# Edge attention on a graph: batches of seven chunks, three buffers of gathered rows, four chunks in one stationary operand

## The chip, the cores and the metric

The kernel runs on one core of a Trainium2 chip. The metric is the device time in microseconds (us), the median of several runs. The engines are named as in the profile: PE is TensorE (PEld its weight loads), DVE is VectorE, ACT is ScalarE, POOL is GpSimd, SP is SyncE. L509 is line 509 of the kernel before.

## What is computed

One attention layer over a graph of 12,500 nodes and 412,500 edges, with 4 heads of 32 columns. The edges come sorted by target node.

```python
h = jnp.maximum(_layernorm(x, axis=-1), 0.0)
h = (h @ W_node.T).reshape(num_nodes, H, HD)             # 12500 x 4 x 32
e = (edge_features @ W_edge.T).reshape(num_edges, H, HD)
h_src = h[src]
h_tgt = h[tgt]
att = jnp.sum(jnp.concatenate([h_src, h_tgt, e], axis=-1) * a, axis=-1)
att = jnp.where(att > 0, att, 0.2 * att)
m = jnp.maximum(segment_max(att, tgt), 0.0)
ex = jnp.exp(att - m[tgt])
denom = segment_sum(ex, tgt) + (num_edges - deg)[:, None] * jnp.exp(-m)
w = ex / denom[tgt]
h_prime = segment_sum(w[:, :, None] * h_src, tgt)
return x + h_prime.reshape(num_nodes, H * HD)
```

The costly part is `h_src`: for each of the 412,500 edges a row of the node table is fetched, weighted by the edge's attention and summed into its target's row.

## The kernel before

First the kernel builds a table in DRAM, one row of 144 f32 values (576 bytes) for each node: four heads of 35 columns (32 features, and columns for sums and maxima, the last of them the source's attention logit) and four logits that the target side uses. Then it goes over the edges.

An edge **chunk** is 896 edges (7 tiles of 128), 461 chunks in all, the last with 3 tiles. A **batch** is CB = 8 chunks (4 pairs), 58 batches in all. The batch loop stands at L775 to L808. In round b it issues, in this order:

- `index(b+2)`: the end points of the edges of a later batch, by a DMA on SP's queue.
- `load(b+1)` (L474 to L502): on SP's queue the edge features `eft` (1792 KB), the edges' targets `mem` (896 KB) and eight small loads `twb` of the target logits.
- `gather(b+1)` (L504 to L512): on POOL, first a copy of one column from `sums` to `gate` (L507), then 56 indirect DMAs (L509), each of which fetches 128 rows of the table into `hs`. There are two buffers of `hs`, for odd and even batches, so the rows of batch b+1 overwrite those of batch b-1. The copy is what makes POOL wait: `sums` is written when the last group of batch b-1 has come out of PE.
- `weigh(b)` (L564 to L592): waits for the rows of batch b. DVE takes the source logits out of `hs` by a transpose (L568), adds them to the logits `z` in PSUM (L576), takes the leaky maximum (ACT L577, DVE L578), runs two scans that find each segment's maximum (L580, L582), ACT takes the exponential (L586), and two transposes (L590, L591) put the weights into PSUM and the maxima back into `hs`.
- `load_pen(b+1)`: penalties that mark segment borders, for the scans.
- `scatter(b)` (L594 to L615): DVE multiplies the rows of each chunk by its weights (L605). Then the sums are matmuls (L613): the stationary operand is a 0/1 membership matrix `hot` of 32 target rows for each of up to G = 3 chunks (128 x 96), the moving one the weighted rows of these chunks (128 x 420), accumulated over 7 tiles into `pa`, of which PSUM holds two buffers. A batch is three groups of 3, 3 and 2 chunks. A group's products between different chunks are not used. In `collect` (L619 to L636) ACT copies the used 32 x 35 pieces out of `pa` (L636), and with the last group of a batch it writes `sums` (L623).
- `begin(b+1)` (L532 to L562): DVE compares the targets (L536), PE computes the logits `z` of the next batch from `eft` (L541, 8 matmuls) and from `mem` and `twb` (L545, 4 matmuls), DVE builds the next `hot` (L549 to L560).
- every two batches `merge` (L638 to L683): DVE joins the two batches' 16 partial results and adds them to `acc`. Some batches also finish a part of the output (L723 to L763). After batch 3 the kernel counts windows (`count_windows`) once.

In the last two batches each group holds one chunk (`step`). Each engine works through its instructions in the order in which they were issued, so POOL issues all gathers of a batch, then meets the next gate. An f32 matmul appears in the trace as two records of PE.

Of the kernel before, what the change touches and what calls it, by code (L numbers as in the profile page):

```python
# [22 lines left out]
K = 64  # L23
# [8 lines left out]
CB = 2 * SB  # L32
NBT = -(-NCH // CB)
NSC = NBT * SB
NC2 = NSC * 2
COLS = NSC * CT
# [4 lines left out]
G = 3  # L41
# [5 lines left out]
R = CB * H  # L47
# [4 lines left out]
ROW = EROW + H  # L52
BUF = max(CE, MC * 2 * AW, CB * H * AW)
# [8 lines left out]
def tiles_of(sc):  # L62

    return [T if c < NCH - 1 else LAST for c in (2 * sc, 2 * sc + 1) if c < NCH]
# [39 lines left out]
def kernel(  # L104
# [41 lines left out]
    nid = const.tile([P, NC2 // 4], F32, name="nid")  # L146
# [10 lines left out]
    left_row = const.tile([1, NSC], F32, name="left_row")  # L157
    down = const.tile([1, NSC], F32, name="down")
    nc.gpsimd.iota(down, pattern=[[-1, NSC]], base=NSC, channel_multiplier=0,
                   allow_small_or_imprecise_dtypes=True)  # L160
# [5 lines left out]
    sums = const.tile([W, 1], F32, name="sums")  # L166
# [12 lines left out]
    def index(b):  # L179
        t = indices.tile([P, SB, 2, CT], I32, name="ends")  # L180
        nc.sync.dma_start(t.rearrange("p j w t -> p (j w t)"), ends[:, b * SB * 2 * CT:(b + 1) * SB * 2 * CT])
        return t


    with (
# [216 lines left out]
        for s in range(2):  # L402
            for j in range(SB):
                at = (2 * j + s) * H
                nc.vector.tensor_copy(wa3[s * K:(s + 1) * K, j, at:at + H], pe[s * K:(s + 1) * K, :])
# [42 lines left out]
        for a in range(4):  # L448
            r = slice(a * W, (a + 1) * W)
            nc.vector.tensor_scalar(nid[r, :].rearrange("p (b k) -> p b k", k=2),  # L450
                                    top[r, :].rearrange("p (b a k) -> p b a k", a=4, k=2)[:, :, a, :], rcol[r, :],
                                    None, op0=OP.add)
# [4 lines left out]
    even = stack.enter_context(tc.tile_pool(name="even", bufs=1))  # L457
# [3 lines left out]
    bank = ps.tile([P, T * R + W + GB * 4 + NC2 // 4], F32, name="exr")  # L461
# [12 lines left out]
    def load(s):  # L474

        c0 = s.b * CB
        s.eft = work.tile([P, SB, CE], F32, name="eft")
        nc.sync.dma_start(s.eft, ef[s.b * SB:(s.b + 1) * SB, :, :].rearrange("j p e -> p j e"))
        s.mem = work.tile([P, 2, CE], F32, name="mem")
        rows = dstc[c0:c0 + CB, :].rearrange("(a k) e -> a (k e)", k=2)  # L480
# [12 lines left out]
        s.tiles = []  # L493
        for t in range(T):
            for sc in range(s.b * SB, (s.b + 1) * SB):
                held = tiles_of(sc) + [0, 0]
                for c in range(2):
                    i = (sc - s.b * SB) * CT + c * T + t
                    if t < held[c]:
                        s.tiles.append(i)  # L500
                    else:
                        nc.vector.memset(s.hs[:, i, :], 0.0)  # L502

    def gather(s, sums=None):  # L504

        if sums is not None:
            nc.gpsimd.tensor_copy(gate[:W, :], sums)  # L507
        for i in s.tiles:
            by_itself(nc.gpsimd.indirect_dma_start(  # L509
                out=s.hs[:, i, :], out_offset=None, in_=table[:, :],  # L510
                in_offset=bass.IndirectOffsetOnAxis(ap=s.ends[:, i // CT, 0, i % CT:i % CT + 1], axis=0)),
                f"rows{s.b}", row_sems, row_done, s.b % ROWSEMS)  # L512
# [14 lines left out]
    def load_pen(s):  # L527
        s.pen = work.tile([R, CE + 1], F32, name="pen")
        rows = pens[s.b * CB:(s.b + 1) * CB, :]
        nc.sync.dma_start(s.pen, rows[:, None, :].to_broadcast([CB, H, CE + 1]))  # L530

    def begin(s):  # L532
# [14 lines left out]
        dk = work.tile([P, SB * CT], I32, name="dk")  # L547
        dst = s.ends[:, :, 1, :]
        nc.vector.tensor_scalar(dk.rearrange("p (j t) -> p j t", t=CT), dst, W - 1, None, op0=OP.bitwise_and)  # L549

        key = work.tile([P, SB * CT], F32, name="key")
        nc.vector.tensor_tensor(
            key.rearrange("p (j c t) -> p j c t", c=2, t=T), dst.rearrange("p j (c t) -> p j c t", t=T),
            floor[:, s.b * CB:(s.b + 1) * CB].rearrange("p (j c) -> p j c", c=2)[:, :, :, None]
            .to_broadcast([P, SB, 2, T]), op=OP.subtract)
        nc.vector.tensor_scalar(key, key, float(W), float(W), op0=OP.is_ge, op1=OP.mult)
        nc.vector.tensor_tensor(key, key, dk, op=OP.add)
        for q0 in range(0, s.chunks, 2):
            k = key[:, q0 * T:q0 * T + CT].rearrange("p (q t) -> p q t", t=T)
            nc.vector.tensor_tensor(hot[:, :, q0:q0 + 2, :].rearrange("p t q r -> p q t r"),  # L560
                                    rows_ps[:, None, None, :].to_broadcast([P, 2, T, W]),
                                    k[:, :, :, None].to_broadcast([P, 2, T, W]), op=OP.is_equal)  # L562

    def weigh(s):  # L564
# [3 lines left out]
        nc.vector.transpose(zst.rearrange("p t i -> p (t i)"),  # L568
                            s.hs[:, :, :EROW].rearrange("p (q t) (h k) -> p t q h k", t=T, h=H)[:, :, :, :, AW - 1])
# [17 lines left out]
        for g in range(NQT):  # L587
# [3 lines left out]
        nc.vector.transpose(s.hs[:, :, :EROW].rearrange("p (q t) (h k) -> p t q h k", t=T, h=H)[:, :, :, :, AW - 1],  # L591
                            both[:, 1, :, :].rearrange("p t r -> p (t r)"))  # L592

    def scatter(s):  # L594


        by_chunk = s.hs[:, :, :EROW].rearrange("p (q t) k -> p q t k", t=T)
        held = [n for j in range(SB) for n in tiles_of(s.b * SB + j)]
        step = G if s.b + 2 < NBT else 1
        for q0 in range(0, s.chunks, step):  # L600
            w = min(step, s.chunks - q0)
            for q in range(q0, q0 + w):
                n = held[q]
                rows = by_chunk[:, q, :n, :].rearrange("p t (h k) -> p t h k", h=H)[:, :, :, :HB]
                nc.vector.tensor_tensor(  # L605
                    rows, rows, ex_ps[:, :n, q * H:(q + 1) * H, None].to_broadcast([P, n, H, HB]), op=OP.mult)
            pa = ps.tile([P, G * H * AW], F32, name="pa", bufs=2)

            n = held[q0 + w - 1]
            order = [0, *range(n, T if w > 1 else n), *range(1, n)]  # L610
            for i in order:
                v = w if i < n else w - 1
                nc.tensor.matmul(pa[:v * W, :v * H * AW], hot[:, i, q0:q0 + v, :].rearrange("p q r -> p (q r)"), by_chunk[:, q0:q0 + v, i, :],  # L613
                                 start=(i == order[0]), stop=(i == order[-1]))
            collect(s, q0, w, pa)  # L615
# [3 lines left out]
    def collect(s, q0, w, pa):  # L619

        first, last = merge_of(s.b)
        if s.b + 2 < NBT and q0 + w == s.chunks:
            nc.scalar.copy(sums, pa[:W, 0:1])  # L623
        if s.b == first and q0 == 0:
# [3 lines left out]
        for q in range(w):  # L628
            at = 1 + (s.b - first) * CB + q0 + q
            for h in range(H):  # L630
                to = merged["r"][h * W:(h + 1) * W, :, at]
                k = (q * H + h) * AW
                if s.b == NBT - 1 and q0 + w == s.chunks and h % 2:
                    nc.vector.tensor_copy(to, pa[q * W:(q + 1) * W, k:k + AW])
                else:
                    nc.scalar.copy(to, pa[q * W:(q + 1) * W, k:k + AW])  # L636
# [138 lines left out]
    with tc.manual_schedule():  # L775
        for b in range(-1, NBT):
# [37 lines left out]
    ps = stack.enter_context(tc.tile_pool(name="rest_ps", bufs=1, space=bass.MemoryType.PSUM))  # L814
    def window():
# [51 lines left out]
        nc.sync.dma_start(eft, ef[ds(sc, 1), :, :].rearrange("o p e -> p (o e)"))  # L867
        by_step = ends.rearrange("p (s w t) -> p s w t", w=2, t=CT)
        src_w = work.tile([P, CT], I32, name="src_w")
        nc.sync.dma_start(src_w, by_step[:, ds(sc, 1), 0, :])  # L870
        dw = work.tile([P, CT], I32, name="dst_w")
        nc.sync.dma_start(dw, by_step[:, ds(sc, 1), 1, :])
# [188 lines left out]
```

## Time and profile before

| what | value |
|---|---|
| runs: median (lowest to highest of 3) | 4826.44 us (4820.51 to 4826.88) |
| the profiled execution's own time | 4815.92 us |
| its span, first to last instruction | 4814.2 us |
| mean granted clock of TensorE | 0.643 |
| PE busy, records | 1946.2 us, 4305 |
| PE weight loads busy | 658.6 us |
| DVE busy | 1805.7 us |
| ACT busy | 719.1 us |
| POOL busy | 3073.5 us |
| matmuls of the sums (L613) | 2526 records, 967.1 us |
| matmuls of the logits (L541 and L545) | 928 and 464 records, 587.0 and 341.2 us |
| multiplying rows by weights (L605) | 461 of 1102 ns |
| gathers (L509) | 3223 of 948 ns |
| DMA traffic | 440.72 MB, mean 92 GB/s |

Lines of the profile are read so: a group's line gives engine, operation, the tiles written and read, the count, busy us and mean ns of one, and then the idle time of the engine just ahead of such instructions with what ended most of it. A timeline's line gives start and duration in us, engine, line, operation, shape and count, and in brackets the idle time before and what ended it.

### The profile page before, as it was taken

How to read it: one execution, taken by the hardware profiler on the slowest of the kernel's cores; microseconds unless marked ns; L12 is line 12 of the kernel's file. 1: busy time of each engine (PE TensorE's matmuls, PEld its weight loads, DVE VectorE, ACT ScalarE, POOL GpSimd, SP SyncE). 2: the span in 40 equal slices, each digit the busy share in tenths (PEclk: the TensorE clock that was granted, in tenths of full speed). 3: DMA queues.
4: the chain of work that ended last, by engine and by line, in shares of the span. 5: the costliest groups of instructions: out<-in, count | busy, mean ns of one | idle time of the engine just before them, and what ended most of it. 6: DMA issues, size and time to landing. Idle time of an engine off the chain costs nothing.

```text
span 4814.2 us, 21409 instructions
## 1 busy us (share of the span) xinstructions
PE 1946.2 (40%) x4305; PEld 658.6 (14%) x4305; DVE 1805.7 (38%) x3337; ACT 719.1 (15%) x2772; POOL 3073.5 (64%) x3333
## 2 busy tenths in 40 slices
PE   5334343433344335343434443434334433443353
PEld 3111111111011111110111111111111111110012
DVE  6242434242334332433343333424342434242425
ACT  5111111110111111111111111111111111110111
POOL 3666666666666666666666666666666666666662
PEclk8566666666666656665656665666566756666666
DMA  6332433333333333333333333333343333333431
GB/s 189 90 88 73 118 79 100 80 103 78 100 83 101 83 95 84 100 79 100 83 95 88 91 88 94 85 94 89 88 95 79 100 80 99 78 104 76 103 81 51
DMA packets 227639, 440.72 MB, mean 92 GB/s; under 512 B 85394, under 2 KB 135566, under 8 KB 227502
## 3 DMA queue, kind: packets, MB, share of 16 engines
q0 software_dynamic: 103136, 237.83, 21.8%
q1 hardware_dynamic: 111038, 194.10, 13.4%
q10 hardware_dynamic: 13328, 7.36, 0.5%
q14 instruction: 100, 0.82, 0.1%
q8 instruction: 37, 0.61, 0.1%
HBM read 423.75 MB, written 15.29 MB: 91 GB/s over the span
## 4 chain that ended last, share of the span: by engine, by line
issue 29%; another core or an unknown queue 27%; PE 22%; DVE 12%; ACT 8%; DMA 1%; DVEq 0%; SPq 0%; ACTq 0%; POOL 0%
PE pa L613 13%; PE z L541 6%; ACT r L636 4%; PE z L545 3%; DVE up L580 2%; DVE m L582 2%; ACT up L749 1%; DVE z L576 1%; ACT a L577 1%; ACT both L586 1%; DVE acc L683 1%; DVE a L583 1%; DVE up L664 1%; DVE hs L605 1%
## 5 line engine op out<-in xcount | busy, mean ns | idle before, releaser
L509 POOL DMA_INDIRECT hs<-table,ends x3223 | 3054.4, 948 | 1037.3 <-issue 1008.5
L613 PE MATMUL pa<-hs,hot 128*96 128x420 f32 (+2 forms) x2526 | 967.1, 549 | 1606.8 <-issue 1184.7
L560 DVE TENSOR_TENSOR hot<-exr,key 128x448 f32<-128x448 f32 x231 | 137.4, 621 | 2460.3 <-remote 2136.4
L541 PE MATMUL z<-eft,wa 128*32 128x384 f32 (+1 forms) x928 | 587.0, 695 | 913.6 <-issue 913.6
L636 ACT COPY r<-pa 32x35 f32<-32x35 f32 x1842 | 385.0, 209 | 2782.7 <-remote 1965.1
L613 PEld LDWEIGHTS pa<-hs,hot 128*96 128x96 f32 (+2 forms) x2526 | 445.1, 181 | 2152.8 <-issue 2044.2
L605 DVE TENSOR_TENSOR hs<-hs,exr 128x924 f32<-128x924 f32 x461 | 476.8, 1102 | 0.0
L545 PE MATMUL z<-mem,twb 128*32 128x512 f32 x464 | 341.2, 826 | 268.1 <-issue 268.1
L507 POOL COPY gate<-sums 32x1 f32<-32x1 f32 x56 | 9.9, 177 | 567.4 <-ACT sums L623 543.0
L541 PEld LDWEIGHTS z<-eft,wa 128*32 128x32 f32 x928 | 104.4, 117 | 1325.4 <-issue 1325.4
L576 DVE TENSOR_TENSOR z<-z,zst 32x224 f32<-32x224 f32 x232 | 89.8, 387 | 162.0 <-PE z L545 74.1
L586 ACT ACTIVATE both<-a 32x224 f32<-32x224 f32 x232 | 89.9, 388 | 370.7 <-DVE a L583 186.7
L536 DVE TENSOR_TENSOR mem<-mem,exr 128x896 f32<-128x896 int32 x116 | 120.4, 1077 | 65.5 <-issue 48.1
L577 ACT ACTIVATE a<-z 32x224 f32<-32x224 f32 x232 | 80.3, 346 | 418.0 <-issue 274.1
L545 PEld LDWEIGHTS z<-mem,twb 128*32 128x32 f32 x464 | 61.2, 134 | 585.3 <-issue 563.3
L683 DVE TENSOR_TENSOR acc<-acc,a 128x70 f32 x461 | 108.5, 235 | 33.8 <-issue 14.5
L580 DVE TENSOR_TENSOR_SCAN up<-pen,z 32x896 f32<-32x896 f32 x58 | 117.0, 2017 | 2.0
L582 DVE TENSOR_TENSOR_SCAN m<-pen,up 32x896 f32<-32x896 f32 x58 | 116.4, 2007 | 2.0
L588 DVE SCALAR_TENSOR_TENSOR both<-pen,m 32x224 f32<-32x224 f32 x232 | 88.7, 382 | 7.1 <-issue 4.8
L749 ACT COPY up<-a 32x224 f32<-32x224 f32 x208 | 70.7, 340 | 33.6 <-issue 23.3
L578 DVE TENSOR_TENSOR z<-z,a 32x896 f32<-32x896 f32 x58 | 63.0, 1087 | 24.5 <-issue 12.6
L583 DVE TENSOR_TENSOR a<-z,m 32x896 f32<-32x896 f32 x58 | 62.5, 1078 | 2.0
(142 smaller groups left out, 726.0 us busy)
## 6 DMA issues: line engine op xcount, KB each, us to landing
eft<-in_ef SPq DMA_DIRECT2D x58, 1792.0 KB
mem<-in_dstc SPq DMA_DIRECT2D x58, 896.0 KB
hs<-table,ends POOLq DMA_INDIRECT x3223
twb<-table SPq DMA_DIRECT2D x464, 0.5 KB
pen<-pens SPq DMA_DIRECT2D x58, 112.1 KB
table<-rows ACTq DMA_DIRECT2D x9, 648.0 KB
xg<-in_x SPq DMA_DIRECT2D x13, 448.0 KB
out<-xg SPq DMA_DIRECT2D x13, 448.0 KB
```

Source lines behind the costliest of these rows:

```text
L509: by_itself(nc.gpsimd.indirect_dma_start(out=s.hs[:, i, :], out_offset=None, in_=table[:, :], in_offset=bass.IndirectOffsetOnAxis(ap=s.end ...
L541: nc.tensor.matmul(s.z[:, part], wa3[:, j, :], s.eft[:, j, part], start=(j == 0), stop=False)
L545: nc.tensor.matmul(s.z[:, part], twb[:, s.b % 2, k, :], s.mem[:, k, part], start=False, stop=(k == 1))
L560: nc.vector.tensor_tensor(hot[:, :, q0:q0 + 2, :].rearrange("p t q r -> p q t r"), rows_ps[:, None, None, :].to_broadcast([P, 2, T, W]), k ...
L576: nc.vector.tensor_tensor(grouped(s.z, g), grouped(s.z, g), zst[g * R:(g + 1) * R, :, :], op=OP.add)
L580: nc.vector.tensor_tensor_scan(up, s.pen[:, :CE], s.z, 0.0, op0=OP.add, op1=OP.max)
L582: nc.vector.tensor_tensor_scan(m[:, ::-1], s.pen[:, CE:0:-1], up[:, ::-1], 0.0, op0=OP.add, op1=OP.max)
L586: nc.scalar.activation(both[g * R:(g + 1) * R, 0, :, :], grouped(att, g), AF.Exp)
L605: nc.vector.tensor_tensor(rows, rows, ex_ps[:, :n, q * H:(q + 1) * H, None].to_broadcast([P, n, H, HB]), op=OP.mult)
L613: nc.tensor.matmul(pa[:v * W, :v * H * AW], hot[:, i, q0:q0 + v, :].rearrange("p q r -> p (q r)"), by_chunk[:, q0:q0 + v, i, :], start=(i ...
L636: nc.scalar.copy(to, pa[q * W:(q + 1) * W, k:k + AW])
L683: nc.vector.tensor_tensor(cols, cols, put[:, i0 + i, :, :], op=OP.add)
```

## The change

A batch becomes CB = 7 chunks, which gives 66 batches. The gathered rows lie in a ring of three buffers instead of two, and `gather(b+1)` now waits for the last group of batch b-2; `sums` exists twice, for even and odd batches. In `hs` the rows are stored tile by tile and within a tile chunk by chunk, so that the seven chunks' rows of one tile are one run of 7 x 144 columns. The seven chunks are summed in two groups with a 128 x 128 stationary operand of four chunks' memberships: group 0 takes chunks 0 to 3, group 1 chunks 3 to 6. Chunk 3 is in both: the moving operand is a contiguous run of 3 x 144 + 70 = 502 columns, which in group 0 ends behind the first two heads of chunk 3, and in group 1 begins with its last two. The one-chunk groups of the last two batches are gone.

The operand rows stay 32 (R), of which a batch now uses 28. The logits are therefore copied out of `hs` into a zeroed tile `logits` before the first transpose, and the last transpose goes into `zst`, from which a second copy fills `hs`. The edge features come in two DMAs (three pairs and one half), and the last matmul of the logits contracts over 64 rows. `pen` is a fixed tile of which 28 rows are loaded. The host lays the edge arrays out by chunk instead of by pair. The code that handles windows left over is changed to fit.

```diff
-CB = 2 * SB
+CB = 2 * SB - 1
-G = 3
+G = 4
+RING = 3
-R = CB * H
+R = 2 * SB * H
+SPLIT = 2 * AW
+RUN = (G - 1) * ROW + SPLIT
...
-    sums = const.tile([W, 1], F32, name="sums")
+    sums = [const.tile([W, 1], F32, name=f"sums{k}") for k in range(2)]
...
-    even = stack.enter_context(tc.tile_pool(name="even", bufs=1))
+    rings = [stack.enter_context(tc.tile_pool(name=f"ring{k}", bufs=1)) for k in range(RING)]
...
-        nc.sync.dma_start(s.eft, ef[s.b * SB:(s.b + 1) * SB, :, :].rearrange("j p e -> p j e"))
+        full = CB // 2
+        nc.sync.dma_start(s.eft[:, :full, :], ef[c0 * K:c0 * K + full * P, :].rearrange("(j p) e -> p j e", p=P))
+        nc.sync.dma_start(s.eft[:K, full, :], ef[c0 * K + full * P:(c0 + CB) * K, :])
...
-        s.hs = (work if s.b % 2 else even).tile([P, SB * CT, ROW], F32, name="hs")
+        s.hs = rings[s.b % RING].tile([P, T * CB, ROW], F32, name="hs")
...
-        for i in s.tiles:
+        for t, q in s.tiles:
             by_itself(nc.gpsimd.indirect_dma_start(
-                out=s.hs[:, i, :], out_offset=None, in_=table[:, :],
-                in_offset=bass.IndirectOffsetOnAxis(ap=s.ends[:, i // CT, 0, i % CT:i % CT + 1], axis=0)),
+                out=s.hs[:, t * CB + q, :], out_offset=None, in_=table[:, :],
+                in_offset=bass.IndirectOffsetOnAxis(ap=s.ends[:, q, 0, t:t + 1], axis=0)),
...
-                nc.tensor.matmul(s.z[:, part], wa3[:, j, :], s.eft[:, j, part], start=(j == 0), stop=False)
+                n = P if 2 * j + 1 < CB else K
+                nc.tensor.matmul(s.z[:, part], wa3[:n, j, :], s.eft[:n, j, part], start=(j == 0), stop=False)
...
-        nc.vector.transpose(zst.rearrange("p t i -> p (t i)"),
-                            s.hs[:, :, :EROW].rearrange("p (q t) (h k) -> p t q h k", t=T, h=H)[:, :, :, :, AW - 1])
+        own = s.hs[:, :, :EROW].rearrange("p (t q) (h k) -> p t q h k", t=T, h=H)[:, :, :, :, AW - 1]
+        nc.vector.tensor_copy(logits[:, :, :CB * H].rearrange("p t (q h) -> p t q h", h=H), own)
+        nc.vector.transpose(zst.rearrange("p t i -> p (t i)"), logits.rearrange("p t i -> p (t i)"))
...
-        nc.vector.transpose(s.hs[:, :, :EROW].rearrange("p (q t) (h k) -> p t q h k", t=T, h=H)[:, :, :, :, AW - 1],
-                            both[:, 1, :, :].rearrange("p t r -> p (t r)"))
+        nc.vector.transpose(zst.rearrange("p t r -> p (t r)"), both[:, 1, :, :].rearrange("p t r -> p (t r)"))
+        nc.vector.tensor_copy(own, zst[:, :, :CB * H].rearrange("p t (q h) -> p t q h", h=H))
...
-        step = G if s.b + 2 < NBT else 1
-        for q0 in range(0, s.chunks, step):
+        flat = s.hs.rearrange("p i c -> p (i c)")
+        for g in range(2):
...
-            pa = ps.tile([P, G * H * AW], F32, name="pa", bufs=2)
+            q0 = g * (G - 1)
+            pa = ps.tile([P, RUN], F32, name="pa", bufs=2)
+            for t in range(T):
+                at = (t * CB + q0) * ROW + g * SPLIT
+                nc.tensor.matmul(pa, hot[:, t, q0:q0 + G, :].rearrange("p q r -> p (q r)"), flat[:, at:at + RUN],
+                                 start=(t == 0), stop=(t == T - 1))
+            collect(s, g, pa)
...
-        if s.b + 2 < NBT and q0 + w == s.chunks:
-            nc.scalar.copy(sums, pa[:W, 0:1])
+        if g == 1:
+            nc.scalar.copy(sums[s.b % 2], pa[:W, 0:1])
...
-                gather(batch(b + 1), sums if b >= 1 else None)
+                gather(batch(b + 1), sums[b % 2] if b >= 2 else None)
```

More of the change, by code (lines that the diff above doesn't have):

```diff
@@ L402 @@
         for s in range(2):
-            for j in range(SB):
+            for j in range(SB - s):
                 at = (2 * j + s) * H
@@ L594, in scatter @@
     def scatter(s):
-        by_chunk = s.hs[:, :, :EROW].rearrange("p (q t) k -> p q t k", t=T)
-        held = [n for j in range(SB) for n in tiles_of(s.b * SB + j)]
-        step = G if s.b + 2 < NBT else 1
-        for q0 in range(0, s.chunks, step):
[L601 to L606, printed above, removed]
-            pa = ps.tile([P, G * H * AW], F32, name="pa", bufs=2)
[L609 to L615, printed above, removed]
+        by_chunk = s.hs[:, :, :EROW].rearrange("p (t q) k -> p q t k", q=CB)
@@ new lines, in scatter @@
+        flat = s.hs.rearrange("p i c -> p (i c)")
+        for g in range(2):
+            for q in range(G * g, min(G * (g + 1), s.chunks)):
+                rows = by_chunk[:, q, :, :].rearrange("p t (h k) -> p t h k", h=H)[:, :, :, :HB]
+                nc.vector.tensor_tensor(
+                    rows, rows, ex_ps[:, :, q * H:(q + 1) * H, None].to_broadcast([P, T, H, HB]), op=OP.mult)
+            q0 = g * (G - 1)
[5 more added lines that the diff above has]
+            collect(s, g, pa)
```

106 lines of the change are left out of this document (55 added, 51 removed).

## The prediction

> **What bounds the kernel now.** I read the busy times first. No engine is full: POOL is busy 64% of 4814.2 us, PE 40%, VectorE (DVE) 38%. So I looked for the loop that sets the period, starting with POOL's groups and their idle time.
>
> ```profile
> PE 1946.2 (40%) x4305; PEld 658.6 (14%) x4305; DVE 1805.7 (38%) x3337; ACT 719.1 (15%) x2772; POOL 3073.5 (64%) x3333
> ...
> L509 POOL DMA_INDIRECT hs<-table,ends x3223 | 3054.4, 948 | 1037.3 <-issue 1008.5
> ...
> L507 POOL COPY gate<-sums 32x1 f32<-32x1 f32 x56 | 9.9, 177 | 567.4 <-ACT sums L623 543.0
> ```
>
> POOL gathers 3223 times, 0.95 us each and 0.30 us of issue between two, and stands still 567.4 us before the 56 gate copies, 10.1 us each. POOL's timeline around two gates shows one period:
>
> ```profile
> 2103.61 0.18 POOL L507 COPY gate<-sums 32x1 f32<-32x1 f32 x1 [9.24 <-ACT sums L623]
> 2104.42 0.98 POOL L509 DMA_INDIRECT hs<-table,ends  x1 [0.63 <-DVE run L646]
> ...
> 2173.84 0.94 POOL L509 DMA_INDIRECT hs<-table,ends  x1 [0.30 <-issue]
> 2184.39 0.18 POOL L507 COPY gate<-sums 32x1 f32<-32x1 f32 x1 [9.60 <-DVEq L523]
> ```
>
> From gate to gate 80.78 us: 0.81 to the first gather, 69.42 from the first to the 56th (the next start is 1.89 later, then 54 steps of 1.2506), 10.55 from the last gather to the next gate. The second gate is marked DVEq, but the copy reads `sums`, and ACT wrote `sums` 0.07 us earlier: that was the wait. What ACT waited for is PE's group results, and these show the odd thing in this kernel. Timelines of PE and ACT in the same period:
>
> ```profile
> 2133.12 12.88 PE L613 MATMUL pa<-hs,hot 128*96 128x420 f32 x28 [28.43 <-issue]
> ...
> 2146.50 2.64 ACT L636 COPY r<-pa 32x35 f32<-32x35 f32 x12 [17.70 <-PE pa L613]
> 2181.51 2.64 ACT L636 COPY r<-pa 32x35 f32<-32x35 f32 x12 [32.37 <-remote]
> 2184.17 0.15 ACT L623 COPY sums<-pa 32x1 f32<-32x1 f32 x1
> ```
>
> The first group of three chunks reaches ACT 13.4 us after PE begins, the second 35.0 us later, the third 2.7 us after that, and the last two only 7.7 and 10.3 us after the last gather was issued. Batch 4, whose gathers had ended while DVE counted windows, has the same matmuls with no gathers in flight (the last gather, then PE and ACT):
>
> ```profile
> 545.46 0.94 POOL L509 DMA_INDIRECT hs<-table,ends  x1 [0.30 <-issue]
> 543.03 12.62 PE L613 MATMUL pa<-hs,hot 128*96 128x420 f32 x28 [38.02 <-DVE hs L605]
> 554.65 5.30 ACT L636 COPY r<-pa 32x35 f32<-32x35 f32 x24 [19.46 <-remote]
> ```
>
> There all three groups are out within 18 us of PE's start (543.0 to 561.1). So while gathers are issued, the results of all but the first group are held, and they come when the gathers end. The loop is: gate, 56 gathers, release, gate. The lag from the last gather to the release grows with the burst: 6.3 us after the 31 gathers of the last batch, 10.55 after 56, about 16 after the 112 ungated ones at the start, near 0.17 us a gather. The last batch's:
>
> ```profile
> 4739.11 0.94 POOL L509 DMA_INDIRECT hs<-table,ends  x1 [0.30 <-issue]
> 4745.07 1.77 ACT L636 COPY r<-pa 32x35 f32<-32x35 f32 x8 [12.37 <-PE pa L613]
> ```
>
> **The change part by part.**
>
> *Third buffer.* gather(n+3) instead of gather(n+2) now waits for batch n's last group. While PE works on batch n, gather(n+2) runs instead of gather(n+1). But gathers run all the same, and if they hold the last group as they do now, the new gate opens where the old one did: behind the burst in flight. The slack of one batch goes to DVE, which in the steady batches doesn't wait for rows anyway. I price the third buffer at nothing in the steady state, if the hold stays; the rivals price it if not.
>
> *Batch of seven.* The loop becomes 0.81 + 1.89 + 47 x 1.2506 = 61.5 us for 49 gathers, and the release: 10.55 - 7 x 0.17 = 9.4 us, at most the 10.55 of now. So 70.9 to 72.0 us for seven chunks, 10.1 to 10.3 a chunk; now 80.78 / 8 = 10.10. What was fixed per batch (the gate, the release) is shared by fewer chunks. I take 71.0.
>
> *Four chunks in one stationary operand.* Two groups of 7 matmuls of 502 columns for 7 chunks, instead of 21 of 420, 420 and 280 for 8: 1004 columns a chunk against 980. A group costs 12.6 x 502 / 420 = 15.1 us on PE. z keeps its 16 + 8 records of 512 or 384 columns for fewer chunks (768 columns a chunk against 672). PE's columns grow 7%. PE's end matters only through the results. From the first transpose of a batch to PE's start are 16.3 us (batches without a merge), then 15.1 for the first group, then the hold of the second: 35.0 to 38.5 us now. That is 66.4 to 69.9 us from batch to batch if nothing released it earlier; a merge adds 13.4 us of DVE (2103.4 to 2116.8), 79.8 to 83.3. In the batches with a merge the end of the gathers releases first, at 71; in those without, the hold may run out just before. 69.5 is therefore the lower end of this forecast, 72.0 the upper.
>
> *Two added copies (own to `logits`, `zst` to own).* Not in the trace. From below, DVE's 128x34 copy of L660 is 0.32 us, L646's 0.19; from above the strided transpose of the same 224 columns, 0.58 us. The two transposes become contiguous and may fall from 0.57 and 0.58 to the 0.43 us of L590, so the two copies net 0.1 to 0.9 us a batch, 7 to 60 us of DVE in 66 batches. They stand ahead of PE's start, which lies 29 us behind the gate, under 55 us of gathers: hidden. I take nothing. Without that cover: 0.5 x 66 = 33 us.
>
> *DVE's fixed part.* The weighing (scans, maxima, exponentials) of some 11 us runs 66 times instead of 58: 88 us more, DVE 38% to 40%. Hidden likewise. If not hidden: 88 us.
>
> *SP.* eft in two DMAs, 7 small loads instead of 8, one half stationary of z: SP has no wait in the chain (SPq 0%). Nothing. POOL's 3223 gathers and ACT's group copies stay the same in number.
>
> *Start and end.* Gathers 0 to 2 are ungated: from 74.1 us, 147 of them, to about 260 us. gather(3) waits for batch 0: with a release of 9.4, 269 us; gather(4) one period later: 340. If neither gate waits it is 323, with the release of 22 that a longer burst suggests 353. I take 340. From gather(4) to gather(65) are 61 periods: 340 + 61 x 71.0 = 4671. Behind the last gate: 38 gathers and release 55.2 (0.81 + 1.89 + 36 x 1.2506 + 7.5), a merge 13.4, weighing 16.3, a group 15.1, z 9.2, weighing 16.3, a group 15.1, and 22.0 from there to the end (4792.3 to 4814.2 now): 162.6. Each last batch counts one group as exposed, since its second goes beside DVE's work. Span 4834. The profiled execution now took 4815.92 for a span of 4814.2 (+1.7), and the median of the runs stands 10.5 above it (4826.44). Forecast 4834 + 12.2 = 4846, say **4845 us**.
>
> [...] The idle time before the gate is 10.1 us in each period, by the third fence a wait for PE's held results. [...]
>
> **The rivals.**
>
> *B, POOL becomes the bound (chance 0.10).* If no result is held, batch n is done before gather(n+2) ends, the gate never waits, and POOL issues through: 74 + 3223 x 1.2506 = 4105, and the last batches behind it, 75, and 12: about 4190 us. For it: the hold seems to begin only with some 28 pa records pending, and a batch now has 28 where it had 42. Against: the release is at the end of the gathers in every steady batch. [...]
>
> *C, released in part, on the other side (0.18).* The second group is now the last of only two. If its hold ends before the gathers do (now 35.0 to 38.5 us after the first), the gate is passed sooner and the third buffer pays. PE starts 29 us after the gate, first group 15, second 20 to 25: 64 to 69 us a period instead of 71. At 66: 340 + 61 x 66 + 162.6 + 12.2 = 4541 us. It decides from where the second group comes before the last gather plus 8 us, and gives faster below a period of 70.5.
>
> *D, clearly slower (0.12).* If the end of the gathers doesn't release the second group, because its longer matmuls aren't through PE by then, the hold runs to its own end and the chain of DVE and PE sets the period: 16.3 + 15.1 + 38.1 = 69.5 us without a merge, 82.9 with one, mean 76.2: 340 + 61 x 76.2 + 162.6 + 12.2 = 5163 us. It decides from where the hold outlasts the release at 71. If the hold grows with the columns (38.1 x 502 / 420 = 45.5) it is 5614 (76.9 and 90.3, mean 83.6).
>
> **How the numbers follow.** *A, the forecast (0.60)*: the loop stays, periods of 69.5 to 72.0, 4750 to 4910 us. About 0.2% (10 us) is what a measurement of this kernel can tell from no change, so 4816.8 to 4836.1 is "the same": periods of 70.5 to 70.9. Of A I give 0.19 to faster, 0.08 to the same, 0.33 to slower. Faster 0.19 + 0.10 + 0.18 = 0.47, same 0.08, slower 0.33 + 0.12 = 0.45: the sign is open. The range takes in A, most of C (from a period of 64, 4420) and the lower part of D; B and the top of D stay out: 4400 to 5010. A's own range is 4750 to 4910.
>
> **What would show it.** Right: gates every 71 us with some 9 us of idle POOL before each, ACT's second copy of a batch 7 to 10 us after the last gather. B: no idle time before L507, POOL over 70% busy. C: second group's copies before the last gather of the burst. D: gates far behind the last gather (15 us and more), every second period near 80. The copies' prices are read from their two lines. Wrong would be above all that the hold follows the gathers at all: then the gap before the gate goes.

## The result and the profile after

The changed kernel takes **5139.01 us** (5136.11 to 5140.35, four runs) against 4825.97: a ratio of 1.065, 95% interval 1.0632 to 1.0669. The forecast was 4845, the range 4400 to 5010: the time lies above both. The experiments were run in series, each on one chip with the kernel before beside it. In two series PE's results were not held back while gathers were issued, as they are in the profile of before (4165 us for the kernel before, 4206 for the changed one); in all others they came late, so each run below is read beside the kernel before of its own series.

The page of the changed kernel, its busy times and the three groups that answer to those shown of before:

```profile
PE 1711.6 (33%) x3819; PEld 598.4 (12%) x3819; DVE 1959.3 (38%) x3726; ACT 750.3 (15%) x2851; POOL 3080.0 (60%) x3342
...
L511 POOL DMA_INDIRECT hs<-table,ends x3223 | 3058.4, 949 | 1066.5 <-issue 1017.6
L612 PE MATMUL pa<-hs,hot 128*128 128x502 f32 x1848 | 943.6, 675 | 2949.1 <-DVE hs L606 2053.7
...
L509 POOL COPY gate<-sums 32x1 f32<-32x1 f32 x63 | 11.3, 179 | 796.6 <-ACT sums L622 796.6
```

The gathers cost what they cost before (949 ns each against 948). POOL now waits 796.6 us ahead of 63 gates, 12.6 us each, against 10.1 ahead of 56. But the mean hides the form. Of the 62 periods from gate to gate 16 take 67.7 us on the mean and 29 take 70.0 (forecast 71.0), 16 take 91.1, and one, with the counting of windows, 104 (its first gather comes 35 us after its gate). By an estimate from these rows, were the 16 like the 45, the kernel would take 16 x 21.9 = 350 us less, 4789 us. POOL's timeline around the start and the end of one long period (last gather and gate, then last gather and next gate):

```profile
2184.88 0.94 POOL L511 DMA_INDIRECT hs<-table,ends  x1 [0.30 <-issue]
2191.88 0.18 POOL L509 COPY gate<-sums 32x1 f32<-32x1 f32 x1 [6.06 <-ACT sums L622]
...
2252.80 0.95 POOL L511 DMA_INDIRECT hs<-table,ends  x1 [0.30 <-issue]
2280.78 0.18 POOL L509 COPY gate<-sums 32x1 f32<-32x1 f32 x1 [27.04 <-ACT sums L622]
```

The first gate opens 7.0 us after the last gather (forecast 9.4), the second 28.0 us after. ACT, DVE and PE in between (timelines):

```profile
2191.60 0.15 ACT L622 COPY sums<-pa 32x1 f32<-32x1 f32 x1 [32.10 <-remote]
...
2249.65 0.35 ACT L581 ACTIVATE a<-z 32x224 f32<-32x224 f32 x1 [53.00 <-issue]
...
2274.24 3.08 ACT L638 COPY r<-pa 32x35 f32<-32x35 f32 x14 [13.80 <-PE pa L612]
2280.19 0.15 ACT L622 COPY sums<-pa 32x1 f32<-32x1 f32 x1 [2.87 <-PE pa L612]
```

```profile
2213.44 0.41 DVE L573 STREAM_TRANSPOSE zst<-logits 128x224 f32<-128x224 f32 x1 [1.98 <-remote]
2249.17 0.39 DVE L580 TENSOR_TENSOR z<-z,zst 32x224 f32<-32x224 f32 x1 [35.32 <-remote]
```

```profile
2171.23 0.80 PE L548 MATMUL z<-mem,twb 128*32 128x384 f32 x1 [2.32 <-issue]
2174.03 0.80 PE L548 MATMUL z<-mem,twb 128*32 128x384 f32 x1 [2.00 <-issue]
2266.15 13.95 PE L612 MATMUL pa<-hs,hot 128*128 128x502 f32 x28 [91.32 <-DVE hs L606]
```

The gate opens on the last group alone (2191.60). The logits z of the next batch stand behind it in PE's order; PE had taken their last record at 2174.03, but their result is not out yet. The new burst holds it for 57.3 us: DVE needs z at 2213.85 and gets it at 2249.17, 3.6 us before the last gather is issued. SP's queue dates the same thing, since it loads `eft` and `mem` anew as soon as z's matmuls have read them:

```profile
2228.13 0.40 SPq L482 DMA_DIRECT2D eft<-in_ef  x1
...
2249.16 0.58 SPq L486 DMA_DIRECT2D mem<-in_dstc  x1
...
2351.86 0.57 SPq L486 DMA_DIRECT2D mem<-in_dstc  x1
```

From the last group (2191.60) the 16 records of z that read `eft` take 36.5 us, the 8 that read `mem` another 21.0: about one in 2.4 us. So z isn't held until the burst ends; PE works on it slowly, and here that takes nearly the whole burst. Only then can the batch be weighed and summed, 31.0 us from z to `sums`, most of it behind a burst that is over: POOL's 27.04. In the three batches that follow, z is out 8.9 us after the gate, before the young burst has slowed PE (2280.78 and 2289.7), and then twice at most 2 us after it (2350.89 and 2351.86); nothing is lost there. This order of four repeats: 15 of the 16 long periods come every fourth batch, with z 55 to 64 us behind the gate, and the first long one follows the ungated gathers of the start.

A second loss stands at the start. The first gather comes at 103.5 us, 29 us later than before:

```profile
75.72 0.12 POOL L334 MEMSET rows<- 128x16 f32 x1 [1.82 <-ACT rows L333]
103.54 1.11 POOL L511 DMA_INDIRECT hs<-table,ends  x1 [27.70 <-issue]
```

```profile
101.33 1.18 DVE L453 TENSOR_SCALAR nid<-top,rcol 32x132 f32<-32x132 f32 x4
```

POOL was ready at 75.84, but begins when DVE has ended the last step of the preparation. That the first buffer lies in memory which the preparation still uses is argued from the order of these lines, and not shown. It isn't the number of buffers: with two (POOL's timeline in run e2b below) the first gather comes as late.

```profile
102.54 1.11 POOL L511 DMA_INDIRECT hs<-table,ends  x1 [27.68 <-issue]
```

### The profile page after: what moved, and what is told of

The parts are those of the page before. It is cut to its first block, busy times and chain, and to the rows that moved or that the text cites. A ratio compares the mean times of both kernels' runs of the same rounds, so it can differ in the third digit from the quotient of the medians.

```text
span 5138.3 us, 21265 instructions
## 1 busy us (share of the span) xinstructions
PE 1711.6 (33%) x3819; PEld 598.4 (12%) x3819; DVE 1959.3 (38%) x3726; ACT 750.3 (15%) x2851; POOL 3080.0 (60%) x3342
## 5 line engine op out<-in xcount | busy, mean ns | idle before, releaser
L612 PE MATMUL pa<-hs,hot 128*128 128x502 f32 x1848 | 943.6, 675 | 2949.1 <-DVE hs L606 2053.7
L612 PEld LDWEIGHTS pa<-hs,hot 128*128 128x128 f32 x1848 | 403.9, 223 | 3535.6 <-issue 3535.6
L563 DVE TENSOR_TENSOR hot<-exr,key 128x448 f32<-128x448 f32 (+1 forms) x264 | 137.1, 561 | 1774.2 <-remote 1557.1
L509 POOL COPY gate<-sums 32x1 f32<-32x1 f32 x63 | 11.3, 179 | 796.6 <-ACT sums L622 796.6
L544 PE MATMUL z<-eft,wa 128*32 128x512 f32 (+3 forms) x1056 | 434.0, 546 | 18.0 <-DMA eft<-in_ef 18.0
L548 PE MATMUL z<-mem,twb 128*32 128x512 f32 (+1 forms) x528 | 285.2, 624 | 339.2 <-issue 338.8
L538 DVE TENSOR_TENSOR mem<-mem,exr 128x896 f32<-128x896 int32 x132 | 137.4, 1082 | 108.1 <-DMA mem<-in_dstc 60.7
L685 DVE TENSOR_TENSOR acc<-acc,a 128x70 f32 x461 | 107.3, 233 | 159.7 <-DVE acc L685 93.9
L544 PEld LDWEIGHTS z<-eft,wa 128*32 128x32 f32 (+1 forms) x1056 | 94.2, 108 | 360.4 <-issue 360.4
L584 DVE TENSOR_TENSOR_SCAN up<-pen_sb,z 32x896 f32<-32x896 f32 x66 | 133.1, 2016 | 2.3
L586 DVE TENSOR_TENSOR_SCAN m<-pen_sb,up 32x896 f32<-32x896 f32 x66 | 132.5, 2007 | 2.2
L548 PEld LDWEIGHTS z<-mem,twb 128*32 128x32 f32 x528 | 54.4, 113 | 508.9 <-issue 508.3
L592 DVE SCALAR_TENSOR_TENSOR both<-pen_sb,m 32x224 f32<-32x224 f32 x264 | 100.3, 380 | 2.7
L582 DVE TENSOR_TENSOR z<-z,a 32x896 f32<-32x896 f32 x66 | 71.7, 1086 | 27.3 <-ACT a L581 18.6
```

What stands on the lines that cost most here:

```text
L538: nc.vector.tensor_tensor(s.mem[:, k, :], s.mem[:, k, :].bitcast(I32), nid_ps[:, pair:pair + 1].to_broadcast([P, CE]), op=OP.is_equal)
L544: nc.tensor.matmul(s.z[:, part], wa3[:n, j, :], s.eft[:n, j, part], start=(j == 0), stop=False)
L548: nc.tensor.matmul(s.z[:, part], twb[:, s.b % 2, k, :], s.mem[:, k, part], start=False, stop=(k == 1))
L563: nc.vector.tensor_tensor(hot[:, :, q0:q0 + n, :].rearrange("p t q r -> p q t r"), rows_ps[:, None, None, :].to_broadcast([P, n, T, W]), k ...
L584: nc.vector.tensor_tensor_scan(up, s.pen[:, :CE], s.z, 0.0, op0=OP.add, op1=OP.max)
L586: nc.vector.tensor_tensor_scan(m[:, ::-1], s.pen[:, CE:0:-1], up[:, ::-1], 0.0, op0=OP.add, op1=OP.max)
```

## The experiments

Theory Z: the long periods come from z, held by the burst that its own batch's gate lets go. Rivals: the third buffer, the four-chunk groups, or the batch of seven lose by themselves. Besides, what makes PE late at all: the bytes of the gathers, PE's columns, the number of records, or the silence of the other queues? Single runs, unless a range is given.

| run | us | kernel before beside it | mean period, us | long ones (84 or more) |
|---|---|---|---|---|
| changed kernel | 5139 | 4826 | 75.4 | 17 of 62 |
| e2b, two buffers | 5146 | 4809 | 75.4 | 16 of 63 |
| g1, three groups | 5164 | 4823 | 75.6 | 2 of 62 |
| e3b, gate after z | 4983 | 4820 | 72.5 | 1 of 62 |
| f5, idle copies on ACT | 4987 | 4823 | 72.9 | 2 of 62 |
| h2, wait before the second group | 5002 | 4822 | 72.9 | 2 of 62 |
| h3, the same, two buffers | 4931 | 4822 | 72.2 | 1 of 63 |
| e4b, half the columns | 5079 | 4820 | 74.7 | 17 of 62 |
| f2, short rows | 5135 | 4809 | 75.3 | 17 of 62 |
| f1, half the records in the sums | 4905 | 4809 | 71.5 | 4 of 62 |
| f4, half the records in z too | 4754 | 4823 | 69.2 | 0 of 62 |
| e1b, busy load queue | 5773 | 4820 | 85.5 | 31 of 62 |

**The first five runs: no late results.** The first four share a series.

```diff
 e1, in the batch loop, behind the stores:
+                if b + 2 < NBT:
+                    for k in range(14):
+                        nc.sync.dma_start(idle, x[k * P:(k + 1) * P, :D // 2])
 e2:
-RING = 3
+RING = 2
-                gather(batch(b + 1), sums[b % 2] if b >= 2 else None)
+                gather(batch(b + 1), sums[(b - 1) % 2] if b >= 1 else None)
 e3, in begin, behind the matmuls of z (the copy in collect goes to a spare column):
+        nc.scalar.copy(sums[(s.b - 1) % 2], s.z[:W, CE - 1:CE])
 e4:
-                nc.tensor.matmul(pa, hot[:, t, q0:q0 + G, :].rearrange("p q r -> p (q r)"), flat[:, at:at + RUN],
+                nc.tensor.matmul(pa[:, :RUN // 2], hot[:, t, q0:q0 + G, :].rearrange("p q r -> p (q r)"), flat[:, at:at + RUN // 2],
```

> Changed kernel, plus 14 small dummy loads (128 x 64 f32 of x into a spare tile, one after the other) on SP's queue behind each batch's own loads; their data is not used. Theory Q: PE's completions are late only while the gathers are the only DMA traffic (in the trace the load queue is silent from 2149 to 2229 us, the stretch in which they are late). Then with the queue kept busy the second group comes about 10 us after the first, POOL no longer waits at the gate, and the time falls to 4200 to 4500 us. Theory N: the lateness is set by how many PE records are issued while gathers run, whatever other queues do. Then the second group stays 25 to 36 us behind the first and the time stays at 5140 us or a little above.

> Changed kernel with two buffers of rows instead of three, and the gate on the batch before (as in the kernel before); seven chunks and two groups stay. Theory Z (the 23 us lost in every fourth period come from the next batch's logits z, still in PE when the gate opens and then held by the new burst; the third buffer lets PE's work of a batch fall early in a burst): two buffers tie the weighing to the gathers again, every period is 69 to 72 us and the time 4780 to 4900 us. Rival: the loss belongs to batches of seven as such (more fixed work on DVE and PE for each chunk); then 5100 us or more.

> Changed kernel, but the column that opens POOL's gate is copied by ACT from the next batch's logits z (last column), not from the batch's last group, so a burst starts only when z is out as well. Theory Z: the long periods of 93 us vanish, every period is 70 to 73 us, the time 4800 to 4950 us. Rival, that the chain of DVE and PE work sets the long period: waiting for more can only cost, 5140 to 5300 us.

> Changed kernel with the moving operand of the sums cut to 251 of 502 columns (half of the products are left out, and wrong pieces are collected); the number of matmuls stays. Theory N (a number of records): the second group still comes 28 to 36 us behind the first in a burst, and the time stays within 5000 to 5140 us. If PE's lateness goes by columns: 14 to 18 us, no idle time before most gates, 4300 to 4600 us.

Measured: 4202, 4204, 4211 and 4198 us, and the kernel before in the same series 4166. Four unlike edits with one result are no four cures. The changed kernel itself had to be run there.

> The changed kernel, nothing altered, run again beside the kernel before. Theory C (the late completions of PE are a condition of the chip or of the time at which it runs): where the kernel before takes 4166 us, as beside the last four kernels, the changed one takes 4200 us, a ratio of 1.005 to 1.012, and POOL issues its gathers without a pause; where the kernel before takes 4826 us the changed one takes 5139 us again. Rival, that the dummy loads, the second buffer and the later gate each cured the wait: the changed kernel takes 5139 us though the kernel before takes 4166.

Measured: 4206.34 us (4204.88 to 4206.72) beside 4164.78, ratio 1.010, interval 1.0083 to 1.0117, in another series without late results. Its groups and PE's timeline:

```profile
L511 POOL DMA_INDIRECT hs<-table,ends x3223 | 3049.9, 946 | 1000.2 <-issue 994.1 <-DVE acc L685 1.8 <-DVE a L676 1.5
...
L509 POOL COPY gate<-sums 32x1 f32<-32x1 f32 x63 | 12.4, 196 | 0.3
```

```profile
2152.25 13.92 PE L612 MATMUL pa<-hs,hot 128*128 128x502 f32 x28 [37.95 <-DVE hs L606]
2166.10 6.55 PE L544 MATMUL z<-eft,wa 128*32 128x512 f32 x16
2172.58 3.19 PE L548 MATMUL z<-mem,twb 128*32 128x512 f32 x8
```

The same gathers at the same pace, and PE takes all 52 records without a gap. POOL never waits (0.3 us in 63 gates), the periods are 61.35 us on the mean, and the bound is rival B's, forecast at 4190. So the lateness belongs to the series, not to the gathers alone. It is not one of the chip either: the chip of this run showed late results in a later series (e1b, e3b, e4b, 4820 us for the kernel before). Here the edits to waits change nothing beyond 0.2%, and of the 41 us that the change costs, 29 would be the later first gather if the kernel before begins at 74 us here too (there is no trace of it in such a series).

**Holds put in by hand.**

> The kernel before, nothing altered, with a profile. Theory B (where PE's results are not late, POOL's stream of gathers is the only bound, for both kernels): 4165 us, POOL without idle time before its gates beyond 1 us, and the 41 us to the changed kernel stand in the start (147 ungated gathers against 112), the end and the eight further gates (2 us each). Rival: the kernel before still waits at its gates here, less than 10 us a batch, since it has only two buffers.

Measured 4822 us: results were late here, so the expectation, made for a series without, isn't tested. The trace repeats the kernel before (54 periods of 81.2 us). So the next three, which add a hold, add it to one that is there.

```diff
 h2 and h3 (e2 with the same), in scatter; h1 likewise in the kernel before, for batch s.b + 1:
+            k = s.b + RING - 1
+            if g == 1 and k < NBT:
+                held = sum(tiles_of(k * CB + q) for q in range(CB))
+                wait = nc.tensor.wait_ge(row_sems[k % ROWSEMS], row_done[k % ROWSEMS] + (16 * held if RING > 2 else 0), synchronizes=[])
             pa = ps.tile([P, RUN], F32, name="pa", bufs=2)
```

> The kernel before, with one wait added: PE begins the second group of a batch only when the rows of the next batch have landed. It puts in by hand what the profile of before showed (results behind the first group come when the gathers end). Theory A (that hold of the groups, and nothing else, made the kernel before take 4826 us): 0.8 + 69.4 + about 2.5 for the last rows to land + about 9 for two groups = 82 us a batch, 4800 to 4950 us. Rival, something else was slow there as well: well below, 4200 to 4600 us.

> The changed kernel with the same wait added: PE begins the second group of batch n only when the rows of batch n+2 have landed. The logits z, which follow in PE's order, are free then. Theory Z (a hold of the groups alone gives the period that was forecast, and the rest of the 5139 us was the hold of z behind the gate): 61.5 + 2.5 + 6 = 70 us a batch, 4700 to 4900 us. Rival, the hold of the groups alone explains it: 5050 to 5200 us.

> The changed kernel with two buffers of rows and the same wait (for the rows of batch n+1, those in flight). Theory: under a hold of the groups the third buffer is worth nothing, 70 us a batch, within 1% of the run with three buffers. Rival: the third buffer takes the weighing off the gathers' path, and two buffers are 3% or more slower.

Measured: 4993, 5002 and 4931 us. The added wait costs the kernel before 3.5%, above the range expected; with results late in any case, theory A isn't tested by it. But the wait makes the changed kernel 2.7% **faster** (5139 to 5002): 60 periods of 71.5 to 73.5 us, 71.7 at the median, and two long ones near the start. PE now begins its second group and z when the gathers are over, takes them without a gap (14 records in 7.6 us, 16 in 6.6, 8 in 3.2), and z is out 9 us after the gate. That is the forecast's loop and near its period; theory Z holds, though the time lies 100 us above its range. h2 and h3 have the same period, 71.7 us. Of the 70 us between them 31 stand ahead of the last gate (4820.1 us against 4789.5), from the first periods, of which h2 has two long ones (98.6 and 108.2) and h3 one (94.3). The other 40 stand behind it (179.8 against 139.8): with three buffers a gate waits for a batch further back, so one batch more is left when the last gate opens. The rival that the third buffer helps is refuted; in this pair it costs 1.4%, a little more than the 1% expected at most.

**The three of the first series again, with late results.** The edits are those above.

> The kernel with 14 small dummy loads on SP's queue behind each batch's own loads, again; the first time its chip had no late completions at all. Only a run beside a kernel before of 4820 us or so tells: theory Q (late only while the gathers are the sole DMA traffic): 4200 to 4500 us; theory N (a number of PE records in flight while gathers run): 5100 to 5200 us. Beside a kernel before of 4166 us it is 4200 again and tells nothing.

> The kernel whose gate waits for the next batch's z as well, again. Beside a kernel before of 4820 us: theory Z (z held behind the gate by the next burst costs 23 us in every fourth batch): no long period is left, 70 to 74 us each, 4850 to 5000 us. Rival, the long period is the chain of DVE and PE and not z: 5140 us or more. Beside 4166 us: 4211 again.

> The kernel with the moving operand of the sums cut to 251 of 502 columns (half of the products left out), again. Beside a kernel before of 4820 us: theory N (records count, not columns): the second group comes 25 to 36 us behind the first, 4950 to 5140 us. If PE's lateness goes by columns: 12 to 18 us, 4250 to 4600 us. Beside 4166 us: 4200 again.

e3b, 4983 us: a gate that opens later makes the kernel 3% faster. 30 periods take 70.4 us and 31 take 73.5, and the 16 of 91 are gone: theory Z. e4b, 5079: half the columns save 60 us, and the second group stays 16 to 39 us behind the first (14 to 39 in the changed kernel) where a burst runs; columns are not it. e1b, 5773: theory Q is refuted. In the burst from 2175 to 2236 us the load queue is busy (SP issues the 14 loads from 2185 to 2222 us), and the second group still comes at 2237.6, 38.5 us behind the first. But the time misses the range of theory N too. The small loads, which cost nothing in the first series, take SP 31 us a batch here instead of 26, and the next batch's end points are loaded behind them: behind 31 of 63 gates the first gather comes some 11 us late, 318 us in all.

**The parts, and what PE's lateness counts.**

> The changed kernel with two buffers of rows and the gate on the batch before, again; the first time its chip had no late completions. Beside a kernel before of 4820 us: theory Z (with three buffers a batch's PE work slides to the early part of a burst, where z is still in PE when the gate opens; with two it is tied to the rows and falls late in the burst): no long period, 70 us each, 4780 to 4900 us. Rival, batches of seven in two groups lose by themselves: 5050 to 5200 us. Beside 4166 us: 4204 again.

Measured 5146 us, 16 long periods: without the third buffer nothing changes. The rival holds, and what theory Z said of the third buffer is refuted: z is held with two buffers as with three.

```diff
 f1 (hot16 and flat are BF16 views of the same tiles, of which the odd elements are taken):
-                nc.tensor.matmul(pa, hot[:, t, q0:q0 + G, :].rearrange("p q r -> p (q r)"), flat[:, at:at + RUN],
+                nc.tensor.matmul(pa, hot16[:, t, 2 * q0 * W + 1:2 * (q0 + G) * W:2], flat[:, 2 * at + 1:2 * (at + RUN):2],
 f4: f1, and the operands of both matmuls of z likewise
 f2, from the fourth batch on:
-                out=s.hs[:, t * CB + q, :], out_offset=None, in_=table[:, :],
+                out=s.hs[:, t * CB + q, :16], out_offset=None, in_=table.rearrange("n (k c) -> (n k) c", c=16),
```

> The changed kernel, the sums' matmuls on the upper halves of the f32 values read as bf16 (the products lose precision, that is all): one record of PE and one weight load for each matmul instead of two, 14 records in place of 28 a batch, columns as before. Theory N (PE falls behind by the number of its records while gathers run, and z after the groups makes 24 more): the second group comes within 15 us of the first, the gates wait less, 4300 to 4800 us beside a kernel before of 4820. If records don't count: 5050 to 5200 us.

> The changed kernel, from the fourth batch on with the same number of gathers and rows, but 64 bytes of each row instead of 576 (from other places of the table; the other columns keep old values, and the logits from the rows are set to zero). If PE is late because of the bytes that the gathers move: no late results, POOL without waits, 4150 to 4300 us. Theory N' (it is the gathers as such, their instructions and descriptors, not their bytes): 5000 to 5140 us beside a kernel before of 4820.

> As the run with half the records in the sums, and the logits' matmuls z on upper halves as well (less precise, nothing left out): 14 + 12 = 26 PE records a batch against 38 there and 52 in the changed kernel. Theory N (records issued while gathers run are what PE falls behind by, those of z too): faster than the 4905 us of that run, 4350 to 4750 us. If z's records don't count: within 1% of 4905 us. Beside a kernel before of 4166 us it is about 4200 us.

f2, 5135 us: a ninth of the bytes of each gather, and the time is that of the changed kernel (5139). What makes PE late isn't the bytes that the gathers move.

f1, 4905 us, above the 4800 expected, and f4, 4754, just above its 4750: the order is that of the records. Both also cut PE's busy time (f4's matmuls of the sums take 358.7 us against 943.6), but half the columns do that too (548.7 in e4), and saved 60 us in e4b. With 52, 38 and 26 PE records a batch the mean wait from the last gather to the gate is 13.6, 9.7 and 6.4 us. In f1 33 of the 63 gates no longer wait, and ACT's copies behind them come one by one, most of them 1.4 us apart. f4 is below the kernel before, but less precise, so it is no rival to it.

```diff
 f5, in weigh, behind the exponentials:
+        for _ in range(40):
+            nc.scalar.copy(spare[:, 1:2], spare[:, 0:1])
```

> The changed kernel with 40 one-element copies added on ACT in each batch, behind the exponentials, where ACT waits for the first group in any case; their result isn't used. Theory S (while gathers run all engines share one limited rate of instructions, about one in 0.7 us when it is used up, as ACT's copies one in 1.4 us in the run with half the records suggest): PE's results come later still, 5250 us or more. Theory P (each engine has its own limit, PE's is used up by its own records): 5139 us within 0.5%.

Measured 4987 us: faster, which neither theory had. The trace suggests why. ACT's timeline early in a burst, and then at the end of the burst before (its last gather at 2130.74, the gate at 2139.11):

```profile
2164.73 1.62 ACT L592 ACTIVATE both<-a 32x224 f32<-32x224 f32 x4 [6.42 <-issue]
2166.38 2.41 ACT L594 COPY spare<-spare 1x1 f32<-1x1 f32 x11
2169.79 0.19 ACT L594 COPY spare<-spare 1x1 f32<-1x1 f32 x1 [1.00 <-ACT spare L594]
2171.19 0.19 ACT L594 COPY spare<-spare 1x1 f32<-1x1 f32 x1 [1.21 <-ACT spare L594]
2172.59 0.19 ACT L594 COPY spare<-spare 1x1 f32<-1x1 f32 x1 [1.21 <-issue]
```

```profile
2134.62 0.21 ACT L642 COPY r<-pa 32x35 f32<-32x35 f32 x1 [1.19 <-issue]
2136.03 0.21 ACT L642 COPY r<-pa 32x35 f32<-32x35 f32 x1 [1.19 <-issue]
2136.72 0.21 ACT L642 COPY r<-pa 32x35 f32<-32x35 f32 x1 [0.49 <-issue]
...
2138.82 0.15 ACT L626 COPY sums<-pa 32x1 f32<-32x1 f32 x1 [0.49 <-issue]
2139.55 3.07 ACT L642 COPY r<-pa 32x35 f32<-32x35 f32 x14 [0.58 <-issue]
```

Fifteen instructions at 0.2 to 0.4 us, and then one in 1.40 us, until some 5 us after the last gather; then 14 in 3.07 us. So ACT falls behind as PE does, after a number of instructions (15 here; PE after 49 records, the last of them at 2112). PE meanwhile is no later than in the changed kernel: its last records of z come 2.80 us apart in both (2114.35, 2117.16 and 2119.95 here). So ACT's 40 instructions don't slow PE, and theory S is refuted. And a slow ACT writes `sums` a little later, 8.4 us after the last gather instead of 7.0. SP's loads of `mem` show that z is out ahead of the gate or at most 2 us behind it, in all but three batches: this would be e3b's cure by accident.

```diff
 g1, in scatter and collect:
-        for g in range(2):
+        for g in range(3):
+            q0, v = 3 * g, min(3, CB - 3 * g)
...
-                nc.tensor.matmul(pa, hot[:, t, q0:q0 + G, :].rearrange("p q r -> p (q r)"), flat[:, at:at + RUN],
+                nc.tensor.matmul(pa[:v * W, :v * EROW], hot[:, t, q0:q0 + v, :].rearrange("p q r -> p (q r)"),
+                                 by_chunk[:, q0:q0 + v, t, :],
```

> The changed kernel with groups of three chunks as in the kernel before (3, 3 and 1 chunks, 21 matmuls a batch instead of 14); seven chunks and three buffers stay. If the two groups of four chunks brought the long period (two groups leave PE early in the burst, with z behind them): no long period, 4750 to 4900 us. If the batch of seven did (the same z, merge and weighing for fewer chunks): the long period stays and the added records come on top, 5140 to 5400 us.

Measured 5164 us: the time is that of the second theory, the periods are those of neither. The long ones are gone, as in the first, but the other 60 are all 74.0 to 75.3 us (74.6 on the mean), and their gates come 13.6 us after the last gather. So the four-chunk groups shape the loss, and undoing them doesn't win it back. What stays is the batch of seven with its new layout: 74.6 / 7 = 10.66 us a chunk against 81.1 / 8 = 10.14 before, with the same 66 PE records a batch beside 48 steps of gathers instead of 55. Seven chunks alone, with the old layout and both other parts undone, wasn't run.

## Why the prediction was wrong

- **The loop and its bound: right.** Gate, burst, release, gate; the release follows the end of the gathers in 45 of 62 periods, at 67.7 and 70.0 us against 71.0 (the shorter kind lies below the lower end of 69.5). The batch 4 of before, read as free of gathers, still had two of them issued behind PE's start (543.03 to 545.46).
- **The third buffer at nothing: right** in the steady state (5146 without it). It isn't free at the start and the end, as h2 and h3 show.
- **The step that failed: the period of 71.0 for all batches**, which counted the release of the second group as the end of a batch. z stands behind that group in PE, and the gate doesn't wait for it. Whenever z was not out, the next burst held it. The 61 periods averaged 75.15: 253 of the 293 us that the worked-out 4846 lacks (15 long ones 303 over 71.0, the one with the counting of windows 33, the 45 others 83 below it). The rest: 36 at the start, 15 in the tail (177.9 against 162.6), less 11 since the median lies 1 us below the profiled execution here, not 10 above. The 36 are a first gather 29 us later than the 74.1 taken over from before, a first gate that doesn't wait (11 less), and a long first period (18): the gate of gather(4) came at 376 instead of 340.
- **The release at 0.17 us a gather: wrong.** Its own rows don't agree on it: the fence of the last batch shows 5.96 us, not 6.3, and from 56 to 112 gathers the lag grew from 10.55 to about 16, 0.10 a gather. Bursts of 49 gathers gave 6.7 and 8.9 in the short periods, and means of 13.6 (g1) and 6.4 (f4). With the gathers the same, it rises with PE's records a batch: 26, 52, 66.
- **Rival D had the number, 5163, at 0.12, with half the mechanism.** The chain of DVE and PE does set the long periods. But it waits for z, not for the second group, and it comes 16 times in 62 with 91 us, not every second time with 82.9.
- **Rival B was right where results aren't late**: 4206 us against 4190.
- **Copies and DVE's fixed part: hidden, right in the short periods.** The two copies take 0.49 and 0.50 us, the transposes fell from 0.57 and 0.58 to 0.41 each: 0.66 us a batch. In the 16 long periods the cover is gone: the weighing and the second copy (0.50 us, 8 us in all) lie in the 31.0 us from z to `sums`.

## What to carry to other kernels

When a queue's gate is opened by one result, list what still stands behind that result on the same engine: whatever isn't out will meet what the gate lets go. Here a later gate (e3b), or one wait more (h2), made the kernel some 3% faster. And before a wait is mended, run the unchanged kernel in more than one series: the kernel before took 4166 and 4822 us here, and in the first kind of series no edit to this wait could be told from none.

## What the runs showed that was not expected

While the gathers ran, in the series with late results, ACT, PE and DVE each slowed to a fixed pace after some quick instructions: ACT to one copy in 1.40 us (from 0.22), PE to one record in 2.1 to 2.8, DVE's updates of `acc` to one in 1.40 (from 0.27), all near multiples of 0.70. Columns (e4b, 60 us) and bytes (f2, 4 us) hardly mattered, the number of PE's records did (f1, 234 us; f4, 385). In r1 the same gathers left no such trace: the idle time ahead of z's last records (L548) is 16.8 us there and 339.2 in the changed kernel with late results, the wait of `acc` for itself 0.6 and 93.9, and of the 958.1 us ahead of ACT's copies 935.6 are a wait for PE's groups.

What causes it stays open. That each engine has a limit of its own would fit f5, in which 40 more instructions on ACT left PE's last records of z 2.80 us apart, but it is a guess: no run shows such a limit, and none shows why only some series have it.
